# Layer 1 of a four-layer graph network: the two weights on turned h in one 256-column product of three exact passes

## The chip, the cores and the metric

One core of one Trainium2 chip runs the whole program in one launch. The metric is device time in microseconds (us), lower is better. The kernel before was timed three times: 912.66, 912.71 and 913.09 us, so the median is 912.71 us. The execution that was profiled took 912.96 us in its own timing; its span from the first to the last instruction is 911.2 us, so 1.76 us lie around the span.

The engines are named as in the profile: PE is the matrix engine (PEld its weight loads), ACT the scalar engine, DVE the vector engine, POOL the GpSimd engine, SP the engine that only issues transfers. Each engine works through its own list of instructions in order and waits on semaphores for the others.

## The reference

x is 32 batches of 512 nodes with 128 features, adj is a 512 x 512 matrix, most of it zero. Each of four layers normalises x over the features, takes the positive part h, computes something of h, and adds it to x. Only layer 1 is touched. It is a Chebyshev layer with the same matrix as both of its supports:

```python
x1 = einsum('bnf,nw->bwf', h, A);  x2 = 2*einsum('bnf,nw->bwf', x1, A) - h
out = relu(concat([h, x1, x2, x1, x2], -1) @ Theta1 + bias)
x = x + out
```

With Theta1 cut into five 128 x 128 blocks, th0 to th4, this is: own = h (th0 - th2 - th4), once = h (th1 + th3), twice = 2 x1 (th2 + th4), and out = relu(own + (once + twice mixed by A) + bias). The kernel computes it in that form: the own part is a plain product per node, the sum once + twice is called w and goes through A a second time. Both have to keep fp32 accuracy. The combined blocks lie in `th[:, 0]` (own), `th[:, 1]` (once) and `th[:, 2]` (twice).

## The kernel before

**Two kinds of product.** A full fp32 product of 128 columns shows in the trace as two PE records. For products with A the kernel splits both operands: `moving_parts` makes of an fp32 tile a part high (ACT), a part low (POOL) and a part mid (DVE), all of type fp32r, and three fp32r passes, one per part against the matching part of adj (`adj_parts`), add up to the exact product. The scales `UP` and `DOWN` correct for the way in which the parts were made.

**Tiling.** A "q" is a pair of batches (16 of them), b a batch of the pair, and a round r handles the two pairs A = 2r and C = 2r + 1, so there are 8 rounds. In each batch the 512 nodes are four blocks t of 128.

**The steps of a round**, all of them generators or functions inside `layer1`, in the order in which the source calls them. The four compute engines follow the source's order (`tc.manual_schedule`), so a call that comes earlier in the source stands earlier in every engine's queue. Only SP's queue is ordered by the framework.

- `normalised(q)`: eight ACT operations (L285) make h of a pair.
- `turn(q)`: two DVE transposes (L321), then four transfers to DRAM and one back (L328, L330) bring h to feature-major order, `hT`.
- `straighten(q)`: two POOL copies (L974) bring `hT` to node order: `hs`, "turned h", from the pool with tag hT (4 buffers).
- `split_up(q, b)`: `moving_parts` of h (L420 ACT, L421 POOL, L422 DVE), into tiles of the pool "small" (13 buffers).
- `first(q, b)`: x1 turned (`x1T`), 12 fp32r passes of 512 columns (L405), evicted by ACT (L407).
- `weighed(q, b)`: w, one PSUM bank (`p_w`): for each of the four blocks t, an fp32 product of 128 columns of `hs` with `th[:, 1]` and one of `x1T` with `th[:, 2]` (L447). Then ACT makes its high part (L992), DVE its low and mid parts (L993, L994), which lie in wide tiles `w`.
- `mix(r, i)`, for the four blocks i of the result: four fp32 products of `hs` with `th[:, 0]`, the own part (L999), and 12 fp32r passes of 512 columns over `w` (L1003) gather in one bank (`p_l`). DVE scales and adds the bias (L1005), and adds the positive part to x (L1007).

`mix` of round r - 1 runs inside round r, which gives w time to be split. `square` is layer 2's matrix, made by POOL in steps spread over the later rounds, `ln_stats` is the statistics of x for layer 2 (DVE, one ACT operation), and `more` brings in the first steps of layer 2 in the last round.

PSUM has eight banks, handed out in turn, and `bank` waits until the use of that bank eight allocations ago has been read.

Of the kernel before, what the change touches and what calls it, by code (L numbers as in the profile page):

```python
# [9 lines left out]
F32 = mybir.dt.float32  # L10
# [4 lines left out]
OP = mybir.AluOpType  # L15
# [14 lines left out]
def kernel(  # L30
# [117 lines left out]
    def spread(w, n):  # L148
        return w[:, None, :].to_broadcast([P, n, D])
# [250 lines left out]
    def mixed_parts(name, left, right, dst):  # L400

        p = bank(f"p_{name}")
        for part in range(3):
            for t in range(NT):
                nc.tensor.matmul(p, right[part][:, blk(t)], left[part][:, t, :],  # L405
                                 start=(t == 0 and part == 0), stop=(t == NT - 1 and part == 2))
        nc.scalar.activation(dst, p, AF.Copy, scale=UP)  # L407

    def three(name):
        return [small_tile(f"{part}_{name}", F32R) for part in PARTS]  # L410
# [7 lines left out]
    def moving_parts(x, high, low, mid):  # L418

        nc.scalar.activation(high, x, AF.Copy, scale=DOWN)  # L420
        nc.gpsimd.tensor_sub(low, x, high.bitcast(F32))  # L421
        nc.vector.scalar_tensor_tensor(mid, x, 1.0 / UP, high.bitcast(F32), OP.mult, OP.subtract)  # L422

    def scaled_parts(x_low, high, low, mid):

# [13 lines left out]
    def columns(xT):  # L439
        return lambda t: xT[:, blk(t)]  # L440

    def projected(name, *terms):

        p = bank(name)
        for t in range(NT):
            for i, (hT, w) in enumerate(terms):
                nc.tensor.matmul(p[:, blk(t)], hT(t), w, start=(i == 0),  # L447
                                 stop=(i == len(terms) - 1))
        return tiles(p)
# [283 lines left out]
    def late_parts():  # L733

        adj_parts.extend(matrix_tile(f"adj_{part}", F32R) for part in PARTS[:2])
        high, low = adj_parts
        for t in range(NT):
            nc.scalar.activation(high[:, t, :], adj_s[:, t, :], AF.Copy, scale=DOWN)
            tc.keep_in_program_order(nc.gpsimd.tensor_sub(adj_s[:, t, :], adj_s[:, t, :], high[:, t, :].bitcast(F32)))
            yield  # L740
        for out, op, p, q in ((1, OP.add, 1, 3), (2, OP.add, 2, 4), (0, OP.subtract, 0, 2)):
            tc.keep_in_program_order(nc.gpsimd.tensor_tensor(th[:, out, :], th[:, p, :], th[:, q, :], op))
        tc.keep_in_program_order(nc.gpsimd.tensor_scalar(th[:, 2, :], th[:, 2, :], 2.0, None, OP.mult))
        nc.gpsimd.tensor_scalar(th[:, 0, :], th[:, 0, :], 1.0 / UP, None, OP.mult)
# [205 lines left out]
    def layer1(more, square):  # L950


        h, hT, hs, parts, x1, w = {}, {}, {}, {}, {}, {}
        normal, turning = {}, {}

        def normalised(q, n=2 * NT):
            if q >= NQ:
                return
            if q not in normal:
                h[q] = normed_tile(q)  # L960
                normal[q] = normed_steps(q, h[q])
            go(normal[q], n)

        def turn(q, n=3):
            if q >= NQ:
                return
            if q not in turning:
                turning[q] = turn_steps(h[q], f"hT1_{q}", hT)
            go(turning[q], n)

        def straighten(q):
            hs[q] = work.tile([P, 2, N], F32, tag="hT", name=f"hs_{q}", bufs=4)
            for b in range(2):
                nc.gpsimd.tensor_copy(split(hs[q][:, b]), hT[f"hT1_{q}"][:, :, b, :].rearrange("p b (a c) -> p a b c", c=QR))  # L974

        def split_up(q, b):
            if q < NQ:
                parts[q, b] = three(f"h_{q}_{b}")
                moving_parts(h[q][:, b].rearrange("p t f -> p (t f)"), *parts[q, b])

        def first(q, b):
            if q < NQ:
                x1[q, b] = small_tile(f"x1T_{q}_{b}")
                mixed_parts(f"x1T_{q}_{b}", adj_parts, parts[q, b], x1[q, b])

        def weighed(q, b):
            r, j = q // 2, 2 * (q % 2) + b
            if j == 0:
                w[r] = [wide_tile(f"w_{part}_{r}", F32R) for part in PARTS]
            p = projected(f"p_w_{q}_{b}", (columns(hs[q][:, b]), th[:, 1, :]), (columns(x1[q, b]), th[:, 2, :]))  # L990
            high, low, mid = (part.rearrange("p t (w f) -> p t w f", f=D)[:, :, j, :] for part in w[r])
            nc.scalar.activation(high, p, AF.Copy, scale=DOWN)  # L992
            nc.vector.tensor_sub(low, p, high.bitcast(F32))  # L993
            nc.vector.scalar_tensor_tensor(mid, p, 1.0 / UP, high.bitcast(F32), OP.mult, OP.subtract)  # L994

        def mix(r, i):
            p = bank(f"p_l1_{r}_{i}")
            for j in range(4):
                nc.tensor.matmul(p[:, blk(j)], columns(hs[2 * r + j // 2][:, j % 2])(i), th[:, 0, :],  # L999
                                 start=(j == 0), stop=False, skip_group_check=True)  # L1000
            for part in range(3):
                for t in range(NT):
                    nc.tensor.matmul(p, adj_parts[part][:, t, blk(i)], w[r][part][:, t, :],  # L1003
                                     start=False, stop=(part == 2 and t == NT - 1), skip_group_check=True)
            nc.vector.scalar_tensor_tensor(tiles(p), tiles(p), UP, spread(b1, 4), OP.mult, OP.add)  # L1005
            x = xq[r].rearrange("p w b t f -> p (w b) t f")[:, :, i, :]
            nc.vector.scalar_tensor_tensor(x, tiles(p), 0.0, x, OP.max, OP.add)  # L1007

        normalised(0)
        yield  # L1010
        turn(0)
        normalised(1)
        yield
        split_up(0, 0)
        split_up(0, 1)
        first(0, 0)
        straighten(0)
        turn(1)
        for r in range(NQ // 2):
            A, C = 2 * r, 2 * r + 1  # L1020
            last = r == NQ // 2 - 1
            if r == 0:
                first(A, 1)
                split_up(C, 0)
                split_up(C, 1)
                straighten(C)
            else:
                split_up(A, 1)
                straighten(A)
                mix(r - 1, 0)  # L1030
                normalised(C, NT)
                turn(C, 1)
                mix(r - 1, 1)
                normalised(C)
                turn(C)
                mix(r - 1, 2)
                split_up(C, 0)
                go(square, r > 3)
                mix(r - 1, 3)
                split_up(C, 1)  # L1040
                first(A, 1)
            weighed(A, 0)
            weighed(A, 1)
            if last:
                more(0)
            go(square, r > 2)
            first(C, 0)
            normalised(A + 2, NT)
            if last:
                more(1)  # L1050
            if r:
                ln_stats(A - 2)
            else:
                go(own[NQ - 3])
                go(own[NQ - 2])
            first(C, 1)
            if last:
                more(2)
            if r:
                straighten(C)  # L1060
            split_up(A + 2, 0)
            normalised(A + 2)
            go(square, r > 3)
            weighed(C, 0)
            weighed(C, 1)
            ln_stats(C - 2) if r else go(own[NQ - 1])
            go(square, r > 3)
            turn(A + 2)
# [185 lines left out]
    def layers_2_and_3():  # L1254
# [15 lines left out]
        for n in range(B):  # L1270
# [16 lines left out]
                fetch(2, 2)  # L1287
            elif n % 2 and n + 5 < B:
                fetch(2, n // 2 + 3)
            if n in (2, 3):  # L1290
                ln_stats(NQ - 4 + n)
            if n == 12:
                weights_of_3()
            if n == 20:
# [135 lines left out]
```

## Time and profile before

| | us |
|---|---|
| median of three runs | 912.71 |
| profiled execution, own time | 912.96 |
| its span | 911.2 |
| layer 1 on PE, from its first pass at 183.61 to its last at about 450.6 | 267 |
| one middle round (337.56 to 370.59) | 33.03 |
| PE, DVE, ACT, POOL busy in the whole span | 901.1, 669.7, 527.5, 485.6 |

Read the whole program's shares first, then the stretch of one round of layer 1, since the whole-program shares are an average over four different layers. [...]the time that a matmul costs is the distance between the starts of two of them, not its length. For ACT, DVE and POOL the length of one operation on its own is what a successor has to wait for; back to back they overlap by some 0.1 us.

### The profile page before, as it was taken

The numbers are of one execution on the slowest core, as the hardware profiler recorded it, in microseconds if no ns is written. First come the engines' busy times: TensorE is split into PE (matmuls) and PEld (weight loads), VectorE is DVE, ScalarE is ACT, GpSimd is POOL, SyncE is SP. The second block draws the span as 40 slices with busy tenths as digits, with TensorE's granted clock in tenths as the row PEclk, the third lists the DMA queues.
The fourth block names the chain that finished last, engine by engine and source line by source line (L and its number), as shares of the span: only waits on it lengthen the run. The fifth ranks groups of instructions, "written<-read, shape, count | busy, mean of one in ns | idle before, by whom it ended". The sixth has DMA issues, their size and how long they took to land.

```text
span 911.2 us, 15170 instructions
## 1 busy us (share of the span) xinstructions
PE 901.1 (99%) x5432; PEld 774.2 (85%) x5433; DVE 669.7 (74%) x1348; ACT 527.5 (58%) x1156; POOL 485.6 (53%) x435
## 2 busy tenths in 40 slices
PE   8999999999999999999999999999999999999998
PEld 4899999988888888888877777777789999999998
DVE  7888886566656665665767777777698888987775
ACT  5874554343532442452556768876577767666663
POOL 5867999932132163342254445545475555666553
PEclk9999999999999999999999999999999999999999
DMA  9255644123114313212332344455212223222111
GB/s 265 50 167 165 186 122 118 24 71 93 35 59 119 87 31 90 71 46 76 106 120 70 93 126 129 132 147 160 70 48 82 81 82 91 73 70 81 59 36 47
DMA packets 83915, 86.06 MB, mean 94 GB/s; under 512 B 6784, under 2 KB 74624, under 8 KB 83840
## 3 DMA queue, kind: packets, MB, share of 16 engines
q1 hardware_dynamic: 83552, 84.57, 32.8%
q8 instruction: 43, 0.70, 0.3%
q10 hardware_dynamic: 288, 0.52, 0.2%
q14 instruction: 32, 0.26, 0.1%
HBM read 44.17 MB, written 40.89 MB: 93 GB/s over the span
## 4 chain that ended last, share of the span: by engine, by line
PE 92%; ACT 3%; DVE 3%; POOL 1%; issue 0%; DMA 0%; DVEq 0%; POOLq 0%; ACTq 0%
PE p_av L1234 12%; PE p_l L1003 10%; PE p_x1T L405 9%; PE p_score L1212 9%; PE p_msgT L1142 9%; PE p_w L447 6%; PE p_l_c L393 4%; PE p_l L999 3%; PE p_l_a L393 3%; PE p_l_d L393 3%; PE p_g L447 3%; PE p_l L447 3%; PE p_hv L447 3%; PE p_feat L447 3%; PE p_phi L1151 3%; PE p_phi L1152 3%
## 5 line engine op out<-in xcount | busy, mean ns | idle before, releaser
L1234 PEld LDWEIGHTS p_av<-hv,ex 128*128 128x128 f32 x1024 | 119.3, 191 | 3.7 <-POOL ex L1207 1.0
L1234 PE MATMUL p_av<-hv,ex 128*128 128x129 f32 x1024 | 119.8, 274 | 0.8 <-POOL ex L1207 0.8
L421 POOL TENSOR_TENSOR low_feat<-feat,high_feat 128x512 fp32r<-128x512 f32 x32 | 53.9, 1686 | 115.8 <-ACT high_feat L420 111.7
L285 ACT ACTIVATE h<-x,sh,rs 128x128 f32<-128x128 f32 x256 | 102.8, 483 | 11.8 <-DVE sh L257 11.0
L1207 DVE TENSOR_TENSOR ex<-ex,adjTx 128x512 f32<-128x512 f32 x64 | 80.4, 1259 | 35.7 <-ACT ex L1205 34.0
L1207 POOL TENSOR_TENSOR ex<-ex,adjTx 128x512 f32<-128x512 f32 x64 | 98.1, 1551 | 12.2 <-ACT ex L1205 8.1
L1093 ACT ACTIVATE h<-x,sh,rs 128x128 f32<-128x128 f32 x256 | 102.9, 485 | 0.0
L428 POOL TENSOR_TENSOR key<-key 128x512 fp32r<-128x512 f32 x32 | 50.2, 1567 | 97.9 <-DVE key L427 39.8
L421 POOL TENSOR_TENSOR low_h<-h,high_h 128x512 fp32r<-128x512 f32 x32 | 47.1, 1482 | 76.6 <-ACT high_h L420 76.4
L245 DVE BATCH_NORM_STATS2 bn<-x 128x6 f32<-128x256 f32 x244 | 85.9, 417 | 0.0
L407 ACT ACTIVATE x1T<-p_x1T 128x512 f32<-128x512 f32 x32 | 19.0, 594 | 109.4 <-PE p_x1T L405 100.8
L1205 ACT ACTIVATE ex<-ex 128x512 f32<-128x512 f32 x128 | 78.9, 651 | 0.0
L1213 ACT ACTIVATE ex<-p_score 128x512 f32<-128x512 f32 x128 | 74.0, 604 | 1.4 <-PE p_score L1212 1.1
L974 POOL COPY hs<-hT 128x512 f32<-128x512 f32 x32 | 18.6, 612 | 81.5 <-DMA hT<-d_hT 81.3
L432 ACT ACTIVATE high_query<-p_query 128x512 fp32r<-128x512 f32 x32 | 19.2, 599 | 73.8 <-PE p_query L1185 73.8
L422 DVE SCALAR_TENSOR_TENSOR mid_feat<-feat,high_feat 128x512 fp32r<-128x512 f32 x32 | 28.9, 904 | 44.3 <-ACT high_feat L420 44.3
L1212 PE MATMUL p_score<-high_query,key 128*128 128x512 f32 x128 | 50.5, 394 | 0.0
L1212 PE MATMUL p_score<-low_query,key 128*128 128x512 f32 x128 | 50.3, 393 | 0.0
L1212 PE MATMUL p_score<-mid_query,key 128*128 128x512 f32 x128 | 50.3, 393 | 0.0
L447 PE MATMUL p_w<-th,x1T 128*128 128x128 f32 x256 | 49.6, 275 | 0.3 <-ACT x1T L407 0.3
L254 ACT ACTIVATE sd<-bn,eps 128x8 f32<-128x8 f32 x46 | 13.9, 302 | 61.5 <-DVE bn L245 57.4
L447 PE MATMUL p_w<-th,hs 128*128 128x128 f32 x256 | 49.4, 275 | 0.0
(220 smaller groups left out, 2350.4 us busy)
## 6 DMA issues: line engine op xcount, KB each, us to landing
d<-hb SPq DMA_DIRECT2D x128, 128.0 KB, 2.5
hT<-d SPq DMA_DIRECT2D x32, 512.0 KB, 3.4
d_hT<-hb_hT SPq DMA_DIRECT2D x112, 128.0 KB, 2.4
hT<-d_hT SPq DMA_DIRECT2D x28, 512.0 KB, 3.3
x<-in_x_dram SPq DMA_DIRECT2D x32, 256.0 KB, 5.0
out_dram<-x SPq DMA_DIRECT2D x31, 256.0 KB, 2.3
adjT_d<-adj_squares SPq DMA_DIRECT2D x4, 256.0 KB
adj_crossed<-in_adj_dram SPq DMA_DIRECT2D x4, 256.0 KB
```

The costliest lines, as they stand in the source:

```text
L245: nc.vector.bn_stats(st[:, k].rearrange("p e s -> p (e s)"), xt[q][:, b, t : t + 2, :].rearrange("p t f -> p f t"))
L285: nc.scalar.activation(h[:, b, t, :], xt[q][:, b, t, :], AF.Relu, bias=shift[q][:, i : i + 1], scale=scale[q][:, i : i + 1])
L393: nc.tensor.matmul(p[:, i * 2 * D : (i + 1) * 2 * D], a[:, k, blk(i)], b[:, k], start=(first and i == 0 and k == 0), stop=(k == 1), skip_g ...
L405: nc.tensor.matmul(p, right[part][:, blk(t)], left[part][:, t, :], start=(t == 0 and part == 0), stop=(t == NT - 1 and part == 2))
L421: nc.gpsimd.tensor_sub(low, x, high.bitcast(F32))
L447: nc.tensor.matmul(p[:, blk(t)], hT(t), w, start=(i == 0), stop=(i == len(terms) - 1))
L1003: nc.tensor.matmul(p, adj_parts[part][:, t, blk(i)], w[r][part][:, t, :], start=False, stop=(part == 2 and t == NT - 1), skip_group_check= ...
L1093: nc.scalar.activation(h[:, t, :], xt[q][:, b, t, :], AF.Relu, bias=shift[q][:, i : i + 1], scale=scale[q][:, i : i + 1])
L1142: nc.tensor.matmul(p, feats[n][part][:, blk(t)], sq[part][:, t, :], start=(t == 0 and part == 0), stop=(t == NT - 1 and part == 2))
L1207: eng.tensor_mul(split(ex[:, t, :]), split(ex[:, t, :]), crossed(mask[:, t, :]))
L1212: nc.tensor.matmul(p, keys[n][i][:, t, :], query[n][i], start=(i == 0), stop=(i == 2))
L1234: nc.tensor.matmul(po[:, i, : D + 1], ex[:, t, blk(i0 + i)], hv[:, t, :], start=(t == 0), stop=(t == NT - 1))
```

## The change

Turned h is split into three fp32r parts as well, and so is the pair of weights `th[:, 0:2]` (own and once side by side, 256 columns). `weighed` then computes both products of `hs` in one go: for each block t three fp32r passes of 256 columns, and on top of the upper 128 columns the fp32 product of `x1T` with `th[:, 2]`. A batch's result is now 4 x 256 columns, so `weighed` takes two PSUM banks. Of each bank, the upper half of each block is split into the parts of w as before (now in halves), and the own half is evicted by ACT into `hs` itself, over the turned h that it came from. POOL then adds the bias to it. `mix` has no own products any more: its DVE epilogue adds the own part, which it reads from `hs`, in two halves.

The source order is rearranged around it: `split_turned` is new, `straighten(C)`, `turn(A + 2)`, `normalised(A + 2)` come earlier in a round, each `split_up` of the second batch is called after the first batch's `weighed`, and the statistics of a pair come one round later (the last four of them in layer 2). x1T is no longer scaled when it is evicted (the scale moves to the eviction of w).

```diff
     def mixed_parts(name, left, right, dst):
...
-        nc.scalar.activation(dst, p, AF.Copy, scale=UP)
+        nc.scalar.copy(dst, p)
...
+    def fixed_parts(x, high, low, mid):
+
+        nc.scalar.activation(high, x, AF.Copy, scale=DOWN)
+        nc.gpsimd.tensor_sub(x, x, high.bitcast(F32))
+        nc.scalar.activation(low, x, AF.Copy, scale=LOW)
+        nc.gpsimd.tensor_sub(mid, high.bitcast(F32), low.bitcast(F32))
...
-        nc.gpsimd.tensor_scalar(th[:, 0, :], th[:, 0, :], 1.0 / UP, None, OP.mult)
...
+        def split_turned(q, b):
+            hs_parts[q, b] = three(f"hs_{q}_{b}")
+            moving_parts(hs[q][:, b], *hs_parts[q, b])
...
         def weighed(q, b):
...
-            p = projected(f"p_w_{q}_{b}", (columns(hs[q][:, b]), th[:, 1, :]), (columns(x1[q, b]), th[:, 2, :]))
-            high, low, mid = (part.rearrange("p t (w f) -> p t w f", f=D)[:, :, j, :] for part in w[r])
-            nc.scalar.activation(high, p, AF.Copy, scale=DOWN)
-            nc.vector.tensor_sub(low, p, high.bitcast(F32))
-            nc.vector.scalar_tensor_tensor(mid, p, 1.0 / UP, high.bitcast(F32), OP.mult, OP.subtract)
+            ps = [bank(f"p_w_{q}_{b}_{i}") for i in range(2)]
+            for t in range(NT):
+                p = ps[t // 2][:, t % 2 * 2 * D : (t % 2 + 1) * 2 * D]
+                for part in range(3):
+                    nc.tensor.matmul(p, hs_parts[q, b][part][:, blk(t)], th_parts[part],
+                                     start=(part == 0 and t % 2 == 0), stop=False, skip_group_check=True)
+                nc.tensor.matmul(p[:, D:], x1[q, b][:, blk(t)], th[:, 2, :], start=False, stop=True,
+                                 skip_group_check=True)
+            for i, p in enumerate(ps):
+                p = p.rearrange("p (t k f) -> p k t f", t=2, k=2)
+                high, low, mid = (part.rearrange("p t (w f) -> p t w f", f=D)[:, 2 * i : 2 * i + 2, j, :]
+                                  for part in w[r])
+                nc.scalar.activation(high, p[:, 1], AF.Copy, scale=UP * DOWN)
+                nc.vector.scalar_tensor_tensor(low, p[:, 1], UP, high.bitcast(F32), OP.mult, OP.subtract)
+                nc.vector.tensor_sub(mid, p[:, 1], high.bitcast(F32))
+                nc.scalar.activation(tiles(hs[q][:, b])[:, 2 * i : 2 * i + 2, :], p[:, 0], AF.Copy, scale=UP)
+            nc.gpsimd.tensor_add(tiles(hs[q][:, b]), tiles(hs[q][:, b]), spread(b1, NT))
 
         def mix(r, i):
             p = bank(f"p_l1_{r}_{i}")
-            for j in range(4):
-                nc.tensor.matmul(p[:, blk(j)], columns(hs[2 * r + j // 2][:, j % 2])(i), th[:, 0, :],
-                                 start=(j == 0), stop=False, skip_group_check=True)
...
-            nc.vector.scalar_tensor_tensor(tiles(p), tiles(p), UP, spread(b1, 4), OP.mult, OP.add)
+            for k in range(2):
+                pk = tiles(p)[:, 2 * k : 2 * k + 2, :]
+                nc.vector.scalar_tensor_tensor(pk, pk, UP, hs[2 * r + k][:, :, blk(i)], OP.mult, OP.add)
...
         first(0, 0)
+        pair = small_tile("th_high", F32R), small_tile("th_low", F32R)
+        th_parts = pair[0][:, : 2 * D], pair[0][:, 2 * D :], pair[1][:, : 2 * D]
+        fixed_parts(th[:, 0:2, :].rearrange("p k f -> p (k f)"), *th_parts)
         straighten(0)
         turn(1)
+        split_turned(0, 0)
```

The order of a round after the change, for r of 1 to 7 (the source of before is printed above):

```python
straighten(A); mix(r - 1, 0); normalised(C, NT); turn(C, 1)
if r > 1: ln_stats(A - 4)
mix(r - 1, 1); normalised(C); turn(C); split_turned(A, 0)
mix(r - 1, 2); split_turned(A, 1); go(square, r > 3); normalised(A + 2)
mix(r - 1, 3)
if r > 1: ln_stats(C - 4)
first(A, 1); split_up(C, 0); straighten(C)
weighed(A, 0); split_up(C, 1); weighed(A, 1)
split_turned(C, 0); go(square, r > 2); first(C, 0)
split_turned(C, 1); turn(A + 2, 1); first(C, 1)
split_up(A + 2, 0); turn(A + 2); go(square, r > 3)
weighed(C, 0); split_up(A + 2, 1); weighed(C, 1)
go(square, r > 3); first(A + 2, 0)
```

Round 0 has no `mix`; it calls `first(A, 1)`, `split_turned(A, 1)`, `split_up(C, 0)`, `straighten(C)` and then goes on from `weighed(A, 0)`, with layer 0's last statistics in between. The framework keeps an ACT and a DVE reader of one PSUM bank apart: in the list of the built program's waits, each own eviction on ACT waits for the mid part of w of the same bank on DVE.

More of the change, by code (lines that the diff above doesn't have):

```diff
@@ L950, in layer1 @@
     def layer1(more, square):
-        h, hT, hs, parts, x1, w = {}, {}, {}, {}, {}, {}
+        h, hT, hs, parts, hs_parts, x1, w = {}, {}, {}, {}, {}, {}, {}
         normal, turning = {}, {}
@@ L1003, in mix @@
                     nc.tensor.matmul(p, adj_parts[part][:, t, blk(i)], w[r][part][:, t, :],
-                                     start=False, stop=(part == 2 and t == NT - 1), skip_group_check=True)
-            nc.vector.scalar_tensor_tensor(tiles(p), tiles(p), UP, spread(b1, 4), OP.mult, OP.add)
+                                     start=(part == 0 and t == 0), stop=(part == 2 and t == NT - 1))
+            for k in range(2):
+                pk = tiles(p)[:, 2 * k : 2 * k + 2, :]
+                nc.vector.scalar_tensor_tensor(pk, pk, UP, hs[2 * r + k][:, :, blk(i)], OP.mult, OP.add)
             x = xq[r].rearrange("p w b t f -> p (w b) t f")[:, :, i, :]
@@ L1023, in layer1 @@
                 first(A, 1)
+                split_turned(A, 1)
                 split_up(C, 0)
-                split_up(C, 1)
-                straighten(C)
             else:
-                split_up(A, 1)
                 straighten(A)
@@ L1032, in layer1 @@
                 turn(C, 1)
+                if r > 1:
+                    ln_stats(A - 4)
                 mix(r - 1, 1)
@@ L1035, in layer1 @@
                 turn(C)
+                split_turned(A, 0)
                 mix(r - 1, 2)
+                split_turned(A, 1)
+                go(square, r > 3)
+                normalised(A + 2)
+                mix(r - 1, 3)
+                if r > 1:
+                    ln_stats(C - 4)
+                first(A, 1)
                 split_up(C, 0)
[L1038 to L1041, printed above, removed]
+            straighten(C)
             weighed(A, 0)
+            split_up(C, 1)
             weighed(A, 1)
@@ L1045, in layer1 @@
                 more(0)
+            split_turned(C, 0)
             go(square, r > 2)
             first(C, 0)
-            normalised(A + 2, NT)
             if last:
                 more(1)
-            if r:
-                ln_stats(A - 2)
-            else:
+            if r == 0:
+                normalised(A + 2)
                 go(own[NQ - 3])
                 go(own[NQ - 2])
+            split_turned(C, 1)
+            turn(A + 2, 1)
             first(C, 1)
@@ L1058, in layer1 @@
                 more(2)
-            if r:
-                straighten(C)
             split_up(A + 2, 0)
-            normalised(A + 2)
+            turn(A + 2)
             go(square, r > 3)
             weighed(C, 0)
+            split_up(A + 2, 1)
             weighed(C, 1)
-            ln_stats(C - 2) if r else go(own[NQ - 1])
+            if r == 0:
+                go(own[NQ - 1])
             go(square, r > 3)
-            turn(A + 2)
             first(A + 2, 0)
@@ L1289, in layers_2_and_3 @@
                 fetch(2, n // 2 + 3)
-            if n in (2, 3):
-                ln_stats(NQ - 4 + n)
+            if n in (2, 3, 4, 5):
+                ln_stats(NQ - 6 + n)
             if n == 12:
```

## The prediction

> **What bounds the kernel now.** I read the page's shares first, then its chain of work that ended last:
>
> ```profile
> PE 901.1 (99%) x5432; PEld 774.2 (85%) x5433; DVE 669.7 (74%) x1348; ACT 527.5 (58%) x1156; POOL 485.6 (53%) x435
> ...
> PE 92%; ACT 3%; DVE 3%; POOL 1%; issue 0%; DMA 0%; DVEq 0%; POOLq 0%; ACTq 0%
> ```
>
> PE is never without work, so a microsecond less on PE is a microsecond less in all, as long as the others still deliver in time. How much they have in hand, the busy times of two rounds of layer 1 show (stretch, then its length, PE, PEld, DVE, ACT, POOL):
>
> ```profile
> 304.47:337.56 33.09, 33.09 (x193) 28.76 (x192) 20.41 (x37) 13.29 (x30) 14.79 (x16) 1.00 0.24 65
> 337.56:370.59 33.03, 33.03 (x193) 28.76 (x192) 20.07 (x37) 13.30 (x30) 15.36 (x16) 1.00 0.24 64
> ```
>
> PE 33.03 of 33.03 us, DVE 20, ACT 13.3, POOL 15. The list of waits gives PE in all of layer 1 one wait of 0.3 us. What a product costs is read from the distances of starts in PE's timeline:
>
> ```profile
> 346.78 1.10 PE L1003 MATMUL p_l<-w_low,adj_low 128*128 128x512 f32 x4
> 347.72 1.09 PE L1003 MATMUL p_l<-w_mid,adj_mid 128*128 128x512 f32 x4
> 348.65 1.05 PE L999 MATMUL p_l<-th,hs 128*128 128x128 f32 x8
> 349.46 1.18 PE L1003 MATMUL p_l<-w_high,adj_high 128*128 128x512 f32 x4
> ...
> 355.36 0.39 PE L447 MATMUL p_w<-th,x1T 128*128 128x128 f32 x2
> 355.58 0.39 PE L447 MATMUL p_w<-th,hs 128*128 128x128 f32 x2
> ```
>
> Four fp32r passes of 512 columns: 348.65 - 347.72 = 0.93, so 0.2325 us each. An fp32 product of 128 columns (two records): 355.58 - 355.36 = 0.22 us (0.223 over a longer stretch). A whole mix takes 3.70, of which its four own products are 0.89 by the chain; x1T 2.8; a weighed 1.785.
>
> The other engines, from one timeline of all of them:
>
> ```profile
> 353.24 1.29 POOL L421 TENSOR_TENSOR low_h<-h,high_h 128x512 fp32r<-128x512 f32 x1
> 353.90 1.18 DVE L422 SCALAR_TENSOR_TENSOR mid_h<-h,high_h 128x512 fp32r<-128x512 f32 x1
> ...
> 357.12 0.60 ACT L992 ACTIVATE w_high<-p_w 128x512 fp32r<-128x512 f32 x1 [1.13 <-PE p_w L447]
> 357.75 0.69 DVE L993 TENSOR_TENSOR w_low<-p_w,w_high 128x512 fp32r<-128x512 f32 x1 [2.67 <-ACT w_high L992]
> 358.36 0.68 DVE L994 SCALAR_TENSOR_TENSOR w_mid<-p_w,w_high 128x512 fp32r<-128x512 f32 x1
> ...
> 365.59 0.69 DVE L422 SCALAR_TENSOR_TENSOR mid_h<-h,high_h 128x512 fp32r<-128x512 f32 x1 [1.14 <-ACT high_h L420]
> 365.64 1.77 POOL L421 TENSOR_TENSOR low_h<-h,high_h 128x512 fp32r<-128x512 f32 x1 [4.44 <-ACT high_h L420]
> ```
>
> Two things: w goes from ACT to DVE in one direction, with a crossing of 0.03 us (357.72 to 357.75); and mid on DVE and low on POOL, which the same ACT operation releases, hinder each other: the later one takes about 0.5 us more (1.18 for 0.69, or 1.77 for 1.29).
>
> **What the Trainium skill says.** "SBUF — State Buffer", "Who interferes with whom": DVE with two SBUF inputs and GpSimd take turns at a port, the second to start stands still. The trace agrees (1.18 ends 0.55 after POOL's 354.53). "PSUM — Partial Sum Buffer", "PSUM bank collisions raise a hardware error": two engines may not read one bank at once, so software keeps them apart. In the kernel before ACT and DVE read `p_w` one after the other anyway; no run here shows a collision. "TensorE: Matmul & The Clock Gate", table of specifications: ACT, DVE and POOL are strict FIFO. The trace agrees: `high_h` stands behind `x1T`, which waits up to 11.5 us for PE.
>
> **The change, part by part.**
>
> *PE.* Per batch it removes eight fp32 products (four once, four own): 8 x 0.223 = 1.78. It adds twelve passes of 256 columns, which no row shows. "TensorE", "Back-to-back issue gap", gives N/2.4 + 2.5 ns: 109 for 256, but 216 for 512, where the trace has 232. I take 109 + 16 = 0.125, so 1.50. Lower bound 0.1115, the closest spacing of any record with its own weight load here (0.223/2): 1.34. Upper bound 0.2325, if a pass costs the same at half the length: 2.79. Saving per batch 0.28 (bounds 0.44 and -1.01), times 32: **9.0 us less** (14 less to 32 more). A round becomes 33.05 - 1.1 = 31.9. Doubling the banks of a weighed (16 allocations a round for 12) costs nothing: each is read a good ten us before its turn comes.
>
> *ACT, DVE, POOL, work alone.* A half (256 elements) costs 0.37 on ACT (366 ns, L342) and 0.41 on DVE (418 ns, L359). ACT per batch: high of hs 0.62, four halves for one operation 4 x 0.37 - 0.60 = 0.88; together 1.5. DVE: mid of hs 0.69 (up to 1.2 beside POOL), 4 x 0.41 - 1.37 = 0.27, mix 2 x 0.41 - 0.70 = 0.12. POOL: low of hs 1.29 to 1.77, bias 1.28. A round's busy time becomes ACT 19, DVE 25 to 27, POOL 26 with square's steps: below 31.9, so no engine is full by its work.
>
> *The wait that is added.* Each own eviction on ACT waits for mid of w of its bank on DVE, which waits for high on ACT. So ACT is held: 0.37 + 0.41 + 0.41 + 0.37 and three crossings of 0.05 = 1.7 a bank, 3.4 a weighed, and before each first low DVE has a mid_h of 0.7 to 1.2 (split_up just ahead), 0.3 to 0.9 of it not covered. With high_h (0.62) that is 4.3 to 4.9 of ACT's queue for a weighed that PE does in 2.4; four a round: 17 to 20. ACT's other work there: h 2 x 3.18, x1T 4 x 0.6, high of hs 4 x 0.62, statistics 0.6: 11.8. **Held time included, ACT goes from 13.3 to 29 to 31.5 of 31.9.** Behind the own evictions in ACT's queue stand the high parts that PE's next products need.
>
> *One round walked through,* t = 0 at PE's start of weighed(A, 0), durations as above. ACT: x1T(A, 1) to 0.8, high_h(C, 0) to 1.4; DVE mid_h to 2.6; halves of (A, 0) until 5.4; high_h(C, 1) to 6.0; DVE mid_h to 7.2; halves of (A, 1) until 10.0; high of hs(C, 0) to 10.6. POOL: bias(A, 1) 10.0 to 11.3, then low of hs(C, 0), behind DVE's mid, to 13.1. PE: the two weighed to 4.8, first(C, 0) to 7.6, first(C, 1) to 10.4; weighed(C, 0) has its low part at 13.1. **PE stands 2.7 us**; 3.6 if ACT starts 0.9 later, since L254 of ln_stats(C - 4) is now ahead of that x1T and itself waits for DVE behind mix. The same handing over for (C, 0), (C, 1) ends after first(A + 2, 0), so mix(r, 0) gets its second high half 0.4 to 1.4 late. Per round 3.1 to 5.0, taken 3.6, less 1.1 saved: **+2.5, seven rounds +17.5**. In rounds 4 and 5 a step of square (1.03 + 0.62, up to 1.9) stands on POOL between low of hs(C, 0) and (C, 1): about +1.5 each, +3.
>
> *Round 0.* Before, PE starts weighed(0, 0) at 189.25 without a wait. Now ACT makes th_high after x1T (187.35), then POOL 0.77 (128x256, L1169), ACT 0.37, POOL 0.77, and only then the copies of hs (1.17), high 0.6 after the first, low to about 192.6: 3.4 late. The walk's 2.7 follows, then some 2.6 at weighed(1, 1), whose high of hs stands behind eight h operations (3.18), and 1.4 at mix: 10 less 1.1, **+9**.
>
> *Moved.* turn(A + 2) starts eight us earlier in the round; SP issues its five transfers in one piece, where before the fifth waited for turn(C) (a run of five issues took 7.0 us). turn(C) stays, but straighten(C) is needed 10 us earlier: transposes at about t = -5.5, and hT landed 7.2 to 9.4 us after them before (187.0 to 194.2, 248.0 to 257.4), so at 2 to 4. POOL's copies (1.17) then end by 5.1, and behind them stands bias(A, 0), ready at 5.4: covered, but narrowly; without that cover low_h(C, 1) and first(C, 1) slip by what the transfer is later. Two ln_stats go to layer 2, 2 x 2.0 on DVE, which is 76 % busy there: nothing. Layer 2's first steps keep their order: nothing.
>
> Sum against the profiled execution's own time: 912.96 + 17.5 + 3 + 9 = 942.5; that execution lies 0.25 above the median, so **942**.
>
> **Rivals.**
>
> (1) *Faster: the handing over is hidden.* For it: ACT's and POOL's busy time fits, and halves of the first bank can start while PE does the second. It decides at one point: low of hs(C, 0) written within the 10.4 us from the start of weighed(A, 0) to the end of first(C, 1); against it the walk's 13.1. Then 912.7 - 9 + 3.4 (round 0's start) = 907, 899 to 911.
>
> (2) *Half of it.* Mids that don't meet POOL and shorter halves take 1.5 us off each round's waits: 3.6 - 1.5 - 1.1 = 1.0 a round, round 0 +6: 914 to 926, and as little as no change at its lower end.
>
> (3) *The passes don't get cheaper with their length,* 0.2325: PE +32, but a weighed of 3.7 covers most of the handing over; +27 and round 0's +9: 949, to 962.
>
> (4) *POOL becomes full:* 8 x 1.77 + 4 x 1.28 + 2.3 + 7.6 of square = 29 in rounds 4 to 6, with its waits more than PE's 32: 962 to 985.
>
> **Chances.** Main case 0.70 (927 to 958), (1) 0.09, (2) 0.12, (3) 0.05, (4) 0.04. The range 917 to 961 leaves out (1), a third of (2) and (4), 0.17. A measurement here can tell about 0.2 %, 1.8 us, from no change: faster 0.09 is (1), same 0.03 is from (2), slower 0.88 the rest.
>
> **What would show it.** Right: PE busy falls below 98 %, and PE waits at p_w for POOL's low of hs and at p_l for w_high; ACT's hs eviction shows idle ended by DVE's w_mid; rounds of 34 to 36 us, with passes of 256 columns 0.11 to 0.13 apart; POOL th before the first hs copy, and PE standing near 189 to 193. Wrong: rounds below 33 us with no PE waits (rival 1), or passes 0.2 apart (rival 3).

## The result, and the profile after

The changed kernel takes 957.48 us, median of 4 runs (954.92 to 960.07), against 912.90 for the kernel before: **slower by 44.6 us, ratio 1.0484, 95 % interval 1.0453 to 1.0516.** The forecast was 942 (917 to 961): sign and range held, the size was some 15 us short, and the median lies only 3.5 us below the upper end of the range. The profiled execution took 954.92 us, its span 953.1, against 912.96 and 911.2 before.

The profile page after, engines and chain of waits:

```profile
PE 904.4 (95%) x5304; PEld 766.3 (80%) x5305; DVE 720.5 (76%) x1476; ACT 568.2 (60%) x1286; POOL 585.2 (61%) x500
...
PE 41%; DVE 5%; ACT 3%; POOL 2%; issue 1%; DMA 0%; DVEq 0%; POOLq 0%; ACTq 0%
```

PE fell from 99 to 95 % of a longer span. No other engine is above 76 %, so none is full; what PE lost, it lost mostly by waiting. (Its busy time did not fall, 904.4 for 901.1: a record ahead of a stand counts with its whole length, 0.28 us for a pass that costs 0.12, and three stretches at half rate, told of at the end, add to it.) The waits are in the list of PE's waits (waiting line, releaser: us in all, times, longest), of which the kernel before had 0.3 us in layer 1:

```profile
PE p_w L1006 <- POOL low_hs L421: 22.3, 12, 2.2
PE p_x1T L405 <- POOL low_h L421: 6.1, 6, 1.1
PE p_w L1006 <- ACT high_hs L420: 4.3, 3, 1.6
PE p_l L1024 <- ACT w_high L1014: 3.1, 4, 0.9
PE p_w L1008 <- ACT x1T L407: 2.3, 3, 0.9
```

Each is one part of a split that comes late: mostly low parts, which POOL makes last. The engines in rounds 3 and 4 (stretch, then its length, PE, PEld, DVE, ACT, POOL):

```profile
288.72:325.72 37.00, 32.80 (x177) 27.17 (x176) 27.23 (x54) 18.24 (x46) 20.59 (x17) 1.00 0.27 86
325.72:364.94 39.22, 33.09 (x178) 27.24 (x177) 28.52 (x57) 19.02 (x49) 26.20 (x23) 1.00 0.23 67
```

A round of 33.05 us became 37.0, and 38.1 to 39.2 in rounds 4 to 6, which have square's steps. POOL, 15 us before, has 20.6 to 26.2 of them: far from full. The cheaper product is there, as PE's timeline shows:

```profile
341.32 0.37 PE L1006 MATMUL p_w<-th_high,high_hs 128*128 128x256 f32 x1
341.52 0.28 PE L1006 MATMUL p_w<-th_high,low_hs 128*128 128x256 f32 x1
341.64 0.28 PE L1006 MATMUL p_w<-th_low,mid_hs 128*128 128x256 f32 x1
341.76 0.38 PE L1008 MATMUL p_w<-th,x1T 128*128 128x128 f32 x2
341.90 0.36 PE L1006 MATMUL p_w<-th_high,high_hs 128*128 128x256 f32 x1
```

Passes start 0.12 us apart where nothing interferes (341.52, 341.64, 341.76), a block of a weighed is 0.58 us (341.32 to 341.90), so a weighed of four blocks is some 2.3.

**The chain in one round.** All engines in round 3, where weighed(A, 0) starts at 303.84:

```profile
305.94 0.30 ACT L254 ACTIVATE sd<-bn,eps 128x8 f32<-128x8 f32 x1 [3.37 <-DVE bn L245]
306.15 0.57 ACT L407 COPY x1T<-p_x1T 128x512 f32<-128x512 f32 x1
...
310.19 0.38 ACT L1017 ACTIVATE hs<-p_w 128x256 f32<-128x256 f32 x1 [0.82 <-DVE w_mid L1016]
310.48 0.63 ACT L420 ACTIVATE high_h<-h 128x512 fp32r<-128x512 f32 x1
310.72 1.29 POOL L1018 TENSOR_TENSOR hs<-hs,b 128x512 f32<-128x512 f32 x1 [0.50 <-ACT hs L1017]
...
311.98 1.72 POOL L421 TENSOR_TENSOR low_h<-h,high_h 128x512 fp32r<-128x512 f32 x1
...
313.33 0.38 ACT L1017 ACTIVATE hs<-p_w 128x256 f32<-128x256 f32 x1 [1.95 <-DVE w_mid L1016]
...
314.81 0.39 ACT L1017 ACTIVATE hs<-p_w 128x256 f32<-128x256 f32 x1 [0.82 <-DVE w_mid L1016]
315.09 0.63 ACT L420 ACTIVATE high_hs<-hs 128x512 fp32r<-128x512 f32 x1
315.34 1.28 POOL L1018 TENSOR_TENSOR hs<-hs,b 128x512 f32<-128x512 f32 x1 [1.64 <-ACT hs L1017]
...
316.57 3.41 POOL L421 TENSOR_TENSOR low_hs<-hs,high_hs 128x512 fp32r<-128x512 f32 x2
```

Read it downwards. Each own eviction on ACT waits for DVE's w_mid; high_h(C, 1) and high_hs(C, 0) stand behind it; POOL's bias, released by the same eviction, goes ahead of the low part that PE needs. PE stands at 313.75 for low_h and at 318.34 for low_hs:

```profile
313.75 1.20 PE L405 MATMUL p_x1T<-adj_low,low_h 128*128 128x512 f32 x4 [1.05 <-POOL low_h L421]
318.34 0.39 PE L1006 MATMUL p_w<-th_high,low_hs 128*128 128x256 f32 x1 [2.19 <-POOL low_hs L421]
327.21 0.73 PE L1024 MATMUL p_l<-w_high,adj_high 128*128 128x512 f32 x2 [0.85 <-ACT w_high L1014]
```

### The profile page after: what moved, and what is told of

Its sections match the earlier page's. It is cut to its first block, busy times and chain, and to the rows that moved or that the text cites. A ratio compares the mean times of both kernels' runs of the same rounds, so it can differ in the third digit from the quotient of the medians.

```text
span 953.1 us, 15376 instructions
## 1 busy us (share of the span) xinstructions
PE 904.4 (95%) x5304; PEld 766.3 (80%) x5305; DVE 720.5 (76%) x1476; ACT 568.2 (60%) x1286; POOL 585.2 (61%) x500
## 4 chain that ended last, share of the span: by engine, by line
PE 41%; DVE 5%; ACT 3%; POOL 2%; issue 1%; DMA 0%; DVEq 0%; POOLq 0%; ACTq 0%
PE p_av L1267 12%; PE p_score L1245 8%; PE p_msgT L1175 6%; PE p_hv L454 3%; PE p_l L454 2%; PE p_query L1218 2%; PE p_phi L1184 2%; PE p_phi L1185 2%; PE p_feat L454 2%; DVE bn L245 1%; DVE hb L1135 1%; ACT high_feat L420 1%; ACT feat L1164 1%; PE p_l L1024 1%; DVE feat L1163 1%
## 5 line engine op out<-in xcount | busy, mean ns | idle before, releaser
L421 POOL TENSOR_TENSOR low_hs<-hs,high_hs 128x512 fp32r<-128x512 f32 x32 | 51.1, 1611 | 37.7 <-ACT high_hs L420 37.5
L1017 ACT ACTIVATE hs<-p_w 128x256 f32<-128x256 f32 x64 | 24.6, 384 | 78.8 <-DVE w_mid L1016 69.2
L421 POOL TENSOR_TENSOR low_h<-h,high_h 128x512 fp32r<-128x512 f32 x32 | 53.1, 1661 | 29.6 <-ACT high_h L420 24.2
L254 ACT ACTIVATE sd<-bn,eps 128x8 f32<-128x8 f32 x46 | 14.0, 304 | 90.6 <-DVE bn L245 85.4
L1018 POOL TENSOR_TENSOR hs<-hs,b 128x512 f32<-128x512 f32 x32 | 41.3, 1289 | 41.0 <-ACT hs L1017 36.5
L1006 PE MATMUL p_w<-th_high,low_hs 128*128 128x256 f32 x128 | 38.4, 300 | 22.3 <-POOL low_hs L421 22.3
L422 DVE SCALAR_TENSOR_TENSOR mid_feat<-feat,high_feat 128x512 fp32r<-128x512 f32 x32 | 25.5, 798 | 44.3 <-ACT high_feat L420 44.3
L1008 PE MATMUL p_w<-th,x1T 128*128 128x128 f32 x256 | 51.9, 286 | 2.6 <-ACT x1T L407 2.3
L1006 PE MATMUL p_w<-th_high,high_hs 128*128 128x256 f32 x128 | 47.7, 372 | 4.3 <-ACT high_hs L420 4.3
L422 DVE SCALAR_TENSOR_TENSOR mid_hs<-hs,high_hs 128x512 fp32r<-128x512 f32 x32 | 40.4, 1277 | 14.8 <-ACT high_hs L420 14.7
```

Source lines behind the costliest of these rows:

```text
L1006: nc.tensor.matmul(p, hs_parts[q, b][part][:, blk(t)], th_parts[part], start=(part == 0 and t % 2 == 0), stop=False, skip_group_check=True)
```

## The experiments

The theories, in the letters of the expectations: **H**, the own evictions' wait holds ACT, and what stands behind them is late; **P**, POOL's queue makes the low parts late; **R**, the new order of the round costs it by itself. For comparison I read one more number from each trace: the length of an undisturbed round (rounds 2 and 3, from the first w_high product of one mix(r, 0) to the next). In these two rounds none of the kernels has a stretch at half rate, but for th_early, so its round 3 (38.4) is left out.

| kernel | median us | ratio to before (95 %) | round us |
|---|---|---|---|
| before | 912.9 | | 33.05 |
| changed | 957.48 | 1.0484 (1.0453 to 1.0516) | 36.98 |
| th_early | 952.85 | 1.0445 (1.0429 to 1.0461) | 37.0 (round 2) |
| bias_left_out | 944.56 | 1.0346 (1.0332 to 1.0360) | 34.64 |
| own_deferred | 938.04 | 1.0261 (1.0243 to 1.0280) | 34.02 |
| own_first | 934.31 | 1.0227 (1.0213 to 1.0241) | 34.17 |
| own_dve_bias_pool | 932.82 | 1.0217 (1.0203 to 1.0231) | 34.08 |
| parts_once | 925.33 | 1.0133 (1.0112 to 1.0153) | 32.56 |
| own_on_dve | 918.18 | 1.0054 (1.0039 to 1.0069) | 31.84 |
| order_only | 916.48 | 1.0037 (1.0024 to 1.0050) | 33.06 |
| combined | 910.12 | 0.9973 (0.9962 to 0.9983) | 31.96 |
| combined_stats | 909.20 | 0.9958 (0.9944 to 0.9972) | 31.96 |
| combined_round0 | 907.70 | 0.9940 (0.9928 to 0.9952) | 31.96 |
| combined_both | 906.43 | 0.9925 (0.9912 to 0.9937) | 31.97 |

**own_deferred**: the own evictions and their bias are issued later in the program.

```diff
-                nc.scalar.activation(tiles(hs[q][:, b])[:, 2 * i : 2 * i + 2, :], p[:, 0], AF.Copy, scale=UP)
-            nc.gpsimd.tensor_add(tiles(hs[q][:, b]), tiles(hs[q][:, b]), spread(b1, NT))
+            held_own[q, b] = ps         # own_part(q, b) issues both lines
...
             split_turned(C, 0)
+            own_part(A, 0)
+            own_part(A, 1)
...
             first(A + 2, 0)
+            own_part(C, 0)
+            own_part(C, 1)
```

> The same instructions as the changed kernel; only the place of the own evictions (and of the bias behind them) in the queues is later: for A behind the high part of hs(C, 0), for C behind x1T(A + 2, 0). ACT then asks for w_mid when DVE has long written it. Theory H (ACT held by the wait of own eviction for w_mid, with the high parts behind it): own evictions show hardly any idle (69 us before), rounds 1 to 3 fall from 37 to 32 to 34 us, rounds with square to about 36, total 930 to 938. Theory P (POOL too busy: low of hs, bias, square): bias comes even later, the sum on POOL is the same, total 950 or more. Theory R (the moved calls cost it): no change, 955 to 960.

Measured 938.04: 19 of the 44.6 us go with not one instruction less. The own evictions' wait for w_mid falls from 69.2 us to 1.1, and the total is at the upper end of H's range, far from P's 950; but rounds 4 and 5, at 39.7 and 38.7 and each with a stretch at half rate in it, are no shorter than in the changed kernel, where H said 36. It moves ACT's wait and POOL's bias together, so it doesn't yet tell which of the two counts.

**order_only**: the changed order of calls (transposes, statistics, splits of h) with the arithmetic of before, so no split of turned h and no own part.

> The changed kernel's order of calls (and the later statistics) with the products, evictions and mix of the kernel before: one part of the change alone. Theory R: most of the loss is here, 935 to 957. Theories H and P: 912 to 917, rounds 33.0 to 33.2 us, PE without waits in layer 1 except near the start.

Measured 916.48. R falls as the main cause: the order costs 3.6 us, and its rounds are 33.06, as before. In round 0 PE waits 1.46 us for x1T, for 0.31 before; and in layer 2 it waits like this, where before has two waits of 0.7:

```profile
487.40 0.30 ACT L254 ACTIVATE sd<-bn,eps 128x8 f32<-128x8 f32 x1 [2.13 <-DVE bn L245]
...
498.31 1.12 PE L1164 MATMUL p_phi<-msgT,phi 128*128 128x512 f32 x2 [0.67 <-DVE msgT L1291]
...
500.87 1.84 PE L454 MATMUL p_l<-phi,msgT 128*128 128x128 f32 x8 [1.43 <-ACT msgT L1165]
```

L254 of a moved statistic holds ACT for 2.1 us, and msgT comes late for two products. The changed kernel has the same two waits, 0.65 and 1.43. In order_only a stretch at half rate follows them (501.17 to 504.58), which the changed kernel doesn't have there.

**parts_once**: turned h is split for the first batch alone, and every batch takes that batch's parts; this leaves out 31 of 32 splits.

```diff
-            hs_parts[q, b] = three(f"hs_{q}_{b}")
-            moving_parts(hs[q][:, b], *hs_parts[q, b])
+            if (q, b) == (0, 0): ...                 # the same two lines
+            hs_parts[q, b] = hs_parts[0, 0]
```

> Leaves out the splitting of turned h in every batch but the first: all products with turned h use the parts of batch 0 (three operations less per batch: ACT 0.62, POOL 1.3 to 1.8, DVE 0.7 to 1.3 us). The own evictions and their waits stay. Theory P: POOL loses some 6 us a round, PE's waits go, rounds about 32, total 905 to 915. Theory H, strict: the holding of ACT stays, and high_h still stands behind it, rounds 34 or more, total 925 to 935. If H acts only through the high part of hs, which is not there any more, rounds are 32 to 33, total 912 to 922, and round 0 loses less.

Measured 925.33, rounds of 32.56. ACT's wait for w_mid is all there (70.6 us in layer 1, 69.2 in the changed kernel), yet a round has only 0.7 us more than own_on_dve's. So the wait hurts by what stands behind it: the splits of turned h and POOL's low parts. The total agrees with strict H (925 to 935), the rounds with the other reading (32 to 33): what is left against before is not in the rounds, but in round 0, whose first mix still starts 10.4 us later than before, and after layer 1 (2.5 us).

**own_on_dve**: DVE evicts the own half and adds the bias in the same instruction; ACT has no own eviction, POOL no bias.

```diff
-                nc.scalar.activation(tiles(hs[q][:, b])[:, 2 * i : 2 * i + 2, :], p[:, 0], AF.Copy, scale=UP)
-            nc.gpsimd.tensor_add(tiles(hs[q][:, b]), tiles(hs[q][:, b]), spread(b1, NT))
+                nc.vector.scalar_tensor_tensor(tiles(hs[q][:, b])[:, 2 * i : 2 * i + 2, :], p[:, 0], UP,
+                                               spread(b1, 2), OP.mult, OP.add)
```

> The own half is evicted by DVE, right behind w_mid, with scale and bias in the same operation: no crossing to ACT and back, ACT loses 4 x 2 x 0.38 us and POOL 4 x 1.29 us a round, DVE gains 8 x 0.35. Theory H, and P too: rounds of 31.6 to 33 us, total 906 to 922, left over is round 0's start of some 3 to 9. If DVE becomes the bound in their place (it was busy 25 to 27 us of a round): rounds of 34 or more, total above 928.

Measured 918.18: 39.3 us go, and undisturbed rounds are 31.84, which is PE's bare work (forecast 31.9). No standing is left in undisturbed rounds once these two lines are gone. What remains is in round 0, in the square rounds and in layer 2. The next two runs take one line each.

**bias_left_out** leaves out L1018; **own_dve_bias_pool** moves L1017 to DVE (as a multiplication by UP) and keeps L1018 on POOL.

> The changed kernel without the addition of b1 on POOL (L1018): that part of the computation is left out, all else is the same. It takes 4 x 1.29 = 5.2 us a round off POOL's queue and leaves ACT's held time as it was. Theory H (the own eviction on ACT holds what stands behind it): POOL's share is only what the walk did not have, some 1 us a round at first(C, 1) and part of the low parts: 945 to 952. Rival P (POOL's queue is what makes the low parts late, the ACT wait only starts it): most of the 39 us that own_on_dve took off goes: 918 to 930.

> The other half of own_on_dve: the own half is evicted by DVE, without the bias, and POOL adds the bias as in the changed kernel. ACT's wait for w_mid is gone, POOL's queue is as full as in the changed kernel. H: near own_on_dve (918.2), 918 to 926, since ACT hands over on time. P: 940 to 955, since POOL has the same work. If bias_left_out and this one both take off much, the two add up on one chain (ACT's high, then POOL's low) and neither alone is the cause.

Measured 944.56 and 932.82: 12.9 and 24.7 us, together 37.6 of own_on_dve's 39.3. By rounds: 36.98 - 34.64 = 2.34 and 36.98 - 34.08 = 2.90, together 5.24, against 36.98 - 31.84 = 5.14. **Neither theory alone holds.** The two gains add up, which fits two delays in series, ACT's high part and then POOL's low part. P fails, as 918 to 930 did not come (944.56 is even 0.4 under H's 945 to 952); H as I put it fails in the other half, as own_dve_bias_pool is 15 us above own_on_dve, not beside it.

**own_first**: is it ACT's work or its wait? One line of the changed kernel is moved, in each bank.

```diff
+                nc.scalar.activation(tiles(hs[q][:, b])[:, 2 * i : 2 * i + 2, :], p[:, 0], AF.Copy, scale=UP)
                 nc.scalar.activation(high, p[:, 1], AF.Copy, scale=UP * DOWN)
                 nc.vector.scalar_tensor_tensor(low, p[:, 1], UP, high.bitcast(F32), OP.mult, OP.subtract)
                 nc.vector.tensor_sub(mid, p[:, 1], high.bitcast(F32))
-                nc.scalar.activation(tiles(hs[q][:, b])[:, 2 * i : 2 * i + 2, :], p[:, 0], AF.Copy, scale=UP)
```

> The changed kernel with one line moved: in each bank ACT evicts the own half (L1017) ahead of the high part (L1014), not behind DVE's mid. Every instruction stays on its engine, POOL's bias too; only the wait of ACT for w_mid is gone. H (it is that wait, not ACT's 0.38 us of work, that holds what stands behind it): the gain of own_dve_bias_pool, where ACT has neither, 957.5 - 24.7 = 933; 930 to 937. If ACT's work counts too: 940 to 948, since the high parts come 0.38 later in each bank. If neither matters: 955 to 960.

Measured 934.31: 23.2 us by the place of one line, as much as taking the eviction off ACT within 1.5 us. The group of L1017 in the changed kernel (busy us and mean ns, then idle before it and its cause) and PE's first waits in own_first show what went:

```profile
L1017 ACT ACTIVATE hs<-p_w 128x256 f32<-128x256 f32 x64 | 24.6, 384 | 78.8 <-DVE w_mid L1016 69.2
```

```profile
PE p_w L1006 <- POOL low_hs L421: 9.9, 11, 1.5
PE p_x1T L405 <- POOL low_h L421: 5.5, 6, 1.0
PE p_w L1006 <- ACT high_hs L420: 3.1, 2, 1.6
```

ACT's work on this line stays in own_first (25.1 us for 24.6); the 69.2 us of waiting for w_mid are not in its list of waits any more. low_hs falls from 22.3 to 9.9, w_high at mix from 3.1 to 0.3. What is left is mostly low_h with 5.5 and low_hs; POOL's bias stands ahead of both, and in bias_left_out low_h falls from 6.1 to 1.9. This run shows the cause of the ACT part: the crossing back from DVE to ACT in one bank. "PSUM — Partial Sum Buffer" of the Trainium skill, section "PSUM bank collisions raise a hardware error", has software keep two engines off one bank, so a bank is handed on; ACT, DVE, ACT costs two crossings, ACT, ACT, DVE one. The trace agrees: L1017 waits for w_mid, up to 2.0 us.

**th_early**: the parts of th and the first split of turned h ahead of first(0, 0), on the changed kernel.

> The changed kernel with the parts of th and the first split of turned h made ahead of first(0, 0), so that ACT makes them before it waits to evict x1T(0, 0). The start of round 0 alone is touched. In the changed kernel PE stands 1.57 and 1.47 us there and then runs at about half rate until 196.6. H with the clock (standing is paid twice, once as waiting and once as slow products): 957.5 - 3.0 - 3 = 951 to 954. Without the clock's part: 954.5. If the first low part is late for another reason (hT not there, POOL's copies): 957 to 958.

Measured 952.85, within the expectation, but that is luck in part: its premise, that PE ran at half rate until 196.6 in the changed kernel, doesn't hold in the profiled execution, whose passes start 0.12 us apart there at a granted clock of 1.00. The first mix of layer 1 starts at 215.0 for 217.8, so the start of round 0 is worth 2.8 us. PE's stands at the first weighed fall from 3.0 us to 0.5, and a new one of 2.1 comes at first(C, 1). In all the profiled execution is only 2.2 us below the changed kernel's (950.9 for 953.1 of span): it has a fourth stretch at half rate, in round 3 (315.18 to 318.59). The changed kernel's runs spread over 5 us.

**combined**: own_on_dve, th_early and three moves (the second split of turned h in round 0, square's first step, the statistics).

```diff
             split_turned(C, 0)
-            go(square, r > 2)
             first(C, 0)
...
+            split_turned(C, 1)
+            go(square, r > 2)
             if r == 0:
                 normalised(A + 2)
                 go(own[NQ - 3])
                 go(own[NQ - 2])
-            split_turned(C, 1)
...
-                if r > 1:
-                    ln_stats(C - 4)
                 first(A, 1)
                 split_up(C, 0)
+                if r > 1:
+                    ln_stats(C - 4)
...
-            if n in (2, 3, 4, 5):
-                ln_stats(NQ - 6 + n)
+            if n in (2, 5, 8, 11):
+                ln_stats(NQ - 4 + (n - 2) // 3)
```

> own_on_dve with four moves: th's parts and the first split of turned h ahead of first(0, 0); in round 0 the split of (C, 1) ahead of the normalisation of A + 2; the first step of square behind the split of (C, 1), and the second ln_stats of a round behind the split of (C, 0); the four ln_stats of layer 2 at its steps 2, 5, 8, 11 in place of 2 to 5. own_on_dve's PE waits in layer 1 are 6.2 us in round 0 (and slow products after), 3.6 in the square rounds, 1.4 and 0.7 in layer 2. If each goes and none returns elsewhere: 918.2 - 6.2 - 4 - 3.6 - 1.5 = 903, so 901 to 907, faster than before, as PE's saving of 9 us alone would make it (904). Rival: the moved steps come late for their own readers (h of A + 2 in round 0, square's parts, statistics) and half of it returns: 909 to 914.

Measured 910.12, within the rival's 909 to 914: part of the gain came back elsewhere. It is faster than before all the same, and the interval leaves 1 out. Of its PE waits, 1.75 (x1T) and 1.11 (low_h) in round 0 and two of 1.4 in layer 2 were left, so I took those:

**combined_stats** puts ln_stats(A - 2) and ln_stats(C - 2) into the last round of layer 1, and leaves two at layer 2's steps 2 and 3. **combined_round0** issues own[13] and own[14] after weighed(C, 1), and split_up(C, 1) ahead of straighten(C), both in round 0 alone. **combined_both** does both.

> combined with two of the four ln_stats of layer 2 put back into layer 1's last round (behind the split of (C, 1) and behind weighed(C, 1)), as the kernel before has them, the other two at layer 2's steps 2 and 3. combined has two PE waits of 1.4 us for msgT in layer 2 (2.8), the kernel before two of 0.7 (1.3). If a statistic put into layer 2 costs a wait of PE wherever it is put: 910.1 - 1.5 = 908.6, 908 to 909.3. If the waits come from something else: 910 to 911. If layer 1's last round has no room for them: 911 to 913.

> combined with two moves in round 0 alone: the statistics own[13] and own[14] behind weighed(C, 1), so that ACT's L254, which waits for DVE, is not ahead of the eviction of x1T(C, 1) (PE stood 1.75 us); and the split of h(C, 1) ahead of the two copies of turned h(C) on POOL, which wait for their transfer (PE stood 1.11 at low_h). Both stands go, with the 0.3 to 0.4 of refilling each: 910.1 - 3.5 = 906.6, 906 to 908. If one of them only moves on: 908 to 909.5.

> combined_stats and combined_round0 together: 910.1 - 1.5 - 3.5 = 905, so 904 to 907, about what PE's saving of 9 us on the kernel before's 912.7 gives (904). Rival: the two don't add up, 907 to 909.

Measured 909.20, 907.70 and 906.43. The first gains 0.9, at the weak end of its expectation, and its interval overlaps combined's; the trace tells why: the msgT waits fall from 2.8 to 1.4 and the part after layer 1 is 1.7 us shorter (466.2 to 464.5), but layer 1's last mix starts 0.9 later, most of it in the last round and the mixes after it. The second gains 2.4. Together 3.7, with the interval apart from combined's: **906.43 is the fastest version, 6.5 us under the kernel before.** Its page and PE's longest waits:

```profile
PE 892.6 (99%) x5305; PEld 762.3 (84%) x5305; DVE 732.0 (81%) x1540; ACT 549.7 (61%) x1222; POOL 537.1 (59%) x468
```

```profile
PE p_idle L519 <- DVE upto L207: 2.0, 1, 2.0
PE p_l L454 <- ACT msgT L1192: 1.4, 2, 0.7
...
PE p_w L1006 <- DVE mid_hs L422: 0.6, 1, 0.6
```

PE is at 99 % again with 8.5 us less work (901.1 - 892.6), close to the 9 us forecast for the product alone. The gain of the idea was there; the changed kernel hid it under its handing over.

## Why the prediction was right, and by how much not

The comparison is of the two profiled executions, 912.96 and 954.92: +42.0, where the forecast's terms gave +29.5. The measured terms are differences of the starts read for the rounds above.

| term | forecast | measured |
|---|---|---|
| a round's PE work | -1.1 | -1.2 (own_on_dve: 33.05 to 31.84) |
| standing in an undisturbed round | 3.6 (3.1 to 5.0) | 5.14 (36.98 - 31.84), just above its bounds |
| seven rounds, without square | +17.5 | +25.6 |
| square | +3 | +4.6 |
| round 0, with the end of the layer | +9 | +9.8 (first mix 11.7 later, the last three mixes 1.9 shorter) |
| after layer 1 | 0 | +2.0 (span less the start of the last mix: 463.5 to 465.5) |
| sum | +29.5 | +42.0 |

The rounds 1 to 7 take 258.9 us for 228.7, +30.2; rounds 4, 5 and 6 exceed the undisturbed 3.93 by 2.2, 1.1 and 1.3, which is put down to square as 4.6, and leaves 25.6. That is less than 7 x 3.93, since round 1 lost only 0.9 (33.99 us for 33.08); round 7, with a stretch at half rate, lost 5.1. The forecast had neither: it counted one walk seven times. The announced rounds of 34 to 36 us came only in rounds 1 and 7; those between took 37.0 and more. The sign rests on the mechanism; that 957.48 still lies in the range rests on its width.

- *Held: the product.* A pass is 0.117, forecast 0.125 (bounds 0.1115 and 0.2325). Rival 3 is out.
- *Held, for half of it: the mechanism.* own_first shows it with one line: the own evictions' wait on DVE holds ACT, and low of hs comes late at weighed(C, 0). It was written at t = 14.5 (318.34 - 303.84) where the walk had 13.1 and rival 1 needed 10.4.
- *Mis-sized: the standing of a round,* 3.6 for 5.14, by two terms of the walk. First, low_h(C, 1), told there only with "covered, but narrowly": PE stood 1.05 at first(C, 1). The walk had ACT free for high_h(C, 0) at 0.8; it came at 2.8 (306.61), behind L254, whose lateness I had at 0.9. Round 1, the one round from 1 to 7 without a call of ln_stats, shows what this weighs: ACT evicts x1T(A, 1) 0.2 us after PE starts weighed(A, 0), against 2.3 in round 3, low of hs(C, 0) is there at 12.4 against 14.5, PE doesn't stand at first(C, 1), and the round is 3 us shorter. In own_on_dve, where the statistics stand in the same place, round 1 is only 0.2 shorter than the next: so L254's lateness costs time where ACT's queue is held afterwards as well. That is an indication from rounds that differ in their place too; no run took the statistics alone out. And I let the bias pass with "covered", though on POOL it stands ahead of low_h(C, 1): bias_left_out shows it to be worth 2.3 us a round. That share belongs to the forecast's rival 4 in its place, though not in its reason: POOL was at 56 % of an undisturbed round (20.6 of 37.0). Second, a stand costs more than its recorded idle: three stands of 1.05, 2.19 and 0.85 are 4.1, the round lost 5.14, about 0.35 for each. The idle counts from the end of a record, and L1006's records last 0.28 where passes start 0.12 apart. "Perfetto Trace Analysis" of the Trainium skill, section "Tensor Engine Instruction (MATMUL, LD_WEIGHTS)", calls TensorE's end times a model; here it agrees.
- *Mis-sized: the square,* forecast in two rounds and seen in three. In rounds 4 and 5 the forecast's stand is there, 1.5 each at low of hs(C, 1). In round 6 it isn't: what that round has more is a longer wait for x1T (0.92) and a stretch at half rate (433.72 to 437.13), so its 1.3 need not be square's.
- *Held: round 0.* PE stood 1.57 and 1.47 at the first weighed (forecast 3.4), 2.10 (2.7), and 1.34 and 1.47 at weighed(1, 1) (2.6). The 1.4 at mix did not come; a stretch at half rate did (211.85 to 215.26), for which the forecast had no term, so that the sum agrees is luck in part.
- *Wrong: "two ln_stats go to layer 2: nothing".* The part after layer 1 grew by 2.0 us. DVE's 76 % is a mean; L254 on ACT waits for bn, and msgT comes late behind it. order_only has a growth of 2.9 and the same two waits without the new product; combined_stats, which takes two of four out of layer 2, shortens that part by 1.7, and combined_both against combined_round0 by 3.0. The size is not fixed: with the same four statistics own_first and own_dve_bias_pool grow by 1.0, bias_left_out by 4.3. PE's waits there show 0.7 of the 2.0; where the rest lies is open.
- *The median* lies 2.6 above the profiled execution, which was the fastest of its four. The mean granted clock of the four falls from 0.994 to 0.978 as the time rises from 954.92 to 960.07 (see the last section); the forecast had no such term.

Left open: how much of the square rounds is POOL's queue and how much L254, since combined moved both; what L254 ahead of x1T costs the changed kernel by itself; and how much of the late low parts is their meeting with DVE's mid, which makes them 1.7 us long for the 1.29 of one alone, since no run here took it away.

## What to carry to other kernels

A product that gets cheaper pays only if the parts it needs are made in time: count the queue of the engine that splits, waits included, up to the product that reads, and not its busy time. If two engines read one bank, let the one that has two reads do both first, so that the bank is handed on once: here 23 us by the place of one line. What is queued on a half idle engine ahead of a part that PE needs can cost PE time: here four biases of 1.29 us cost a round 2.3. Put such work behind the part, or into an instruction that runs anyway.

## What was not expected of the hardware

**PE ran at half rate for 3.41 us after stretches in which it had stood a good half of the time.** It did so in three places of the changed kernel. Two lines of PE's timeline in round 6, a pass apart, then the 3.41 us before and the 3.41 us of that place (last columns: granted clock, DMA share, GB/s):

```profile
434.52 0.41 PE L1006 MATMUL p_w<-th_high,low_hs 128*128 128x256 f32 x1
434.74 0.41 PE L1006 MATMUL p_w<-th_low,mid_hs 128*128 128x256 f32 x1
```

```profile
430.31:433.72 3.41, 1.41 (x12) 1.41 (x13) 3.41 (x4) 1.45 (x4) 3.41 (x3) 1.00 0.00 0
433.72:437.13 3.41, 3.41 (x19) 3.41 (x18) 2.63 (x6) 0.98 (x3) 1.92 (x2) 0.50 0.29 66
```

Passes are 0.22 apart, for 0.12, and the granted clock is 0.50; the other two places are 211.85 to 215.26 and 471.27 to 474.68. In round 7 the rest of weighed(C, 0), from its first low_hs pass at 470.58 to the next weighed at 474.10, takes 3.52 us; the same stretch in round 3 takes 2.22 (318.34 to 320.56). So this place costs some 1.3.

"TensorE: Matmul & The Clock Gate" of the Trainium skill, section "What's actually happening", has the clock halved after an idle window of about 3.4 us, the windows running freely. That they run freely, the traces show: the three places start 221.87 and 37.55 us apart, which is 65 and 11 times 3.413. In th_early the four (209.37, 315.18, 431.24, 468.78) are 31, 34 and 11 times that apart, in own_on_dve the two (193.27, 210.34) 5 times. That a whole window must be idle, they don't bear out: no stand of the changed kernel was longer than 2.2 us. Cut its time from 150 to 880 us into windows of 3.413 us on that grid: the ones just ahead of the three slow places have 2.0 to 2.3 us of recorded idle on PE, all others 1.8 or less. In the other kernels the window ahead of each slow place in that time has 1.7 to 3.4. So from these traces some half of a window standing was enough, an estimate, since the ends of PE's records are modelled.

This also explains why the same stands don't always bring it on. In round 0 PE stood 1.57 and 1.47 at the first weighed in the changed kernel, and 1.58 and 1.47 in own_on_dve. In the first the two fall into two windows (187.96 to 191.37 and 191.37 to 194.78), and full rate followed; in the second into one (189.86 to 193.27), and passes 0.21 apart followed. Since the grid lies differently in each execution, the changed kernel's spread of 5 us, with a granted clock from 0.994 to 0.978, fits it too, where combined and its variants, which hardly stand, lie within 2; only one execution of each kernel was traced, so that part is not shown.
